# Masked attention over kept tokens: turning x into rows and outputs into columns by VectorE's 32x32 blocks instead of TensorE's transposes

## The chip, the cores and the metric

The kernel runs on one core of one Trainium2 chip. The metric is the device time of one execution in microseconds. Five engines work side by side, each through its own instructions in order: TensorE (PE; its weight loads are listed as PEld), VectorE (DVE), ScalarE (ACT), GpSimd (POOL) and SyncE (SP, which here only issues transfers). They meet through semaphores; transfers run on 16 DMA engines.

## The reference

x has 8 batches of D = 512 features by T = 1024 tokens, float32; the mask keeps about half of the tokens; Wq and Wo are 512 x 512.

```
xt = transpose(x, (0, 2, 1))
q = xt @ Wq.T                       # queries, keys and values are all q
qh = q in 8 heads of 64
scores = einsum('bhqd,bhkd->bhqk', qh, qh) / sqrt(64)
logits = (scores * cmask + (1 - cmask) * -1e30) * rmask
ctx = softmax(logits) @ qh
out = x + transpose(ctx @ Wo.T, (0, 2, 1))
```

A row whose query is masked has only zeros as logits, so its output is the mean over all tokens and the same for each such row of a batch.

## The kernel before

The path taken is `attention_of_kept_tokens` (L319). Per batch it packs the kept tokens into NK = 576 columns (five chunks of keys, c = 0..4, the last of 64; the last column stands for the mean of all tokens), computes attention on those alone, and spreads the results to all 1024 tokens at the end. A second function for masks that keep too much lies beside it and isn't run here.

Packing: `load_batch` (L387) brings x as features by tokens. `turn` (L405) makes 128 tokens into rows with four TensorE transposes into one PSUM bank, a ScalarE copy and a store to the DRAM tensor xd that GpSimd issues; `means` (L420) sums the features with ScalarE. `search` (L442, VectorE) finds for each packed column the token it comes from, `gather` (L458, GpSimd) fetches these rows from xd, `collect` (L471) turns them back to features by tokens (xc) on TensorE.

Attention: a batch has four pairs of heads, pr = 0..3, so there are 32 pairs in a row. For a pair, `project` (L492) makes q in two halves, `values` (L512) turns q into rows v and has VectorE find the largest length, which `bias_of` (L539) makes into the exponent's bias. The main loop (L1031) goes over the pairs, and in each over c: `scores` (L553) issues the score matmuls and ScalarE's exponentials, `add_up` (L583) has VectorE add up the exponentials of chunk c-1. After the last c, `attend` (L615) issues the 40 records of the product with v. In the next pair's c = 0, `invert` (L671) makes 1/sum, writes it to DRAM (row) and reads it back spread over the partitions (rb); `contexts` (L700) multiplies the result cT by rb, at c = 2 if the current pair is pr = 0, later else.

Output: in the next batch, `output` (L710) multiplies by Wo, 128 packed tokens at a time, the four pairs' cT accumulated in one bank in the order of the pairs (L718), so its fourth step needs cT of pr = 3; the rows are stored to DRAM (od). `output` 0 and 1 are tasks of pr = 0, 2 and 3 of pr = 1, 4 of pr = 2. `fetch` (L788, GpSimd) then brings a row of od for each of the 1024 tokens (g), and `finish` (L799) turns four 128 x 128 blocks on TensorE, VectorE adds x (xr, from `load_rest`, L767) and SP stores the sum. The last batch has functions of its own (`begin_output`, `end_output`, `fetch_last`, `finish_tokens`).

The order on each engine is the order in which the program issues work. `tasks_of` (L840) gives each pair a list of further work with rough costs; `mix` (L880) merges a front and a back list, and the loop (L1070) pulls tasks so that each c gets its share:

```
for c in range(NC):
    scores(pair, c)
    if c: add_up(pair, c - 1)
    ...                        # invert, contexts, bias_of, search, gather, loads, fetch
    while todo and ... done < share * (c + 1) - 0.3 ...:
        cost, task = todo.pop(0); task(); done += cost
    issue_stores()
attend(pair)
```

Before, `turn` for the next batch stands in the lists of pr = 0 (five) and pr = 1 (three, first of all), `finish` of the batch before in the list of pr = 3, and `search` in the c loop of pr = 0. PSUM banks for all this come from one ring of four (`bank`, L379); scores have two tiles of two banks.

Of the kernel before, what the change touches and what calls it, by code (L numbers as in the profile page):

```python
# [10 lines left out]
F32 = mybir.dt.float32  # L11
I32 = mybir.dt.int32
AF = mybir.ActivationFunctionType
ALU = mybir.AluOpType
AX = mybir.AxisListType
# [6 lines left out]
Q = 32  # L22
NK = 576
# [295 lines left out]
def attention_of_kept_tokens(ctx, tc, x, mask, wq, wo, out, ident, wqT, woT, verdict, flag):  # L319
# [24 lines left out]
    nc = tc.nc  # L344
    B, D, T = x.shape
    P = 128
    DK = D // NH
    SCALE = 1.0 / math.sqrt(DK)
    ND = D // P
# [2 lines left out]
    NN = T // NB  # L352
    G = NB // P
    A = P // Q
    KH = NK // 2
    sizes = [min(P, NK - c * P) for c in range(-(-NK // P))]
    NC = len(sizes)
# [10 lines left out]
    key = keep.tile([P, NC], F32, name="key")  # L368
    kept = keep.tile([P, B], F32, name="kept")
    origin = keep.tile([P, B, NT], I32, name="origin")  # L370
    pads = keep.tile([P, B, NC], F32, name="pads")
    pens = keep.tile([P, B, NC], F32, name="pens")
    low = keep.tile([P, 2, LAST], F32, name="low")
# [5 lines left out]
    def bank(name):  # L379
        return ps.tile([P, NB], F32, tag="t", name=name, bufs=4)  # L380


    weights = {}
    xs, xbars, xds, xins, xcs, valids, searches = {}, {}, {}, {}, {}, {}, {}
    stores = [[], []]

    def load_batch(b, queue=None):  # L387
        xs[b] = {}
        for r in range(NN):
            for d in range(ND):  # L390
                t = sb.tile([P, NB], F32, tag="x", name=f"x_{b}_{d}_{r}", bufs=NN * ND)
                (queue or nc.sync).dma_start(t, x[b, d * P : (d + 1) * P, r * NB : (r + 1) * NB])
                xs[b][d, r] = t

    def queries_of(b):

# [5 lines left out]
            nc.gpsimd.tensor_copy(part[rows, :], valid[rows, r * KH : (r + 1) * KH])  # L402
        valids[b] = valid, part

    def turn(b, i):  # L405

        r, at = divmod(i * P, NB)
        pt = bank(f"xt_{b}_{i}")
        for d in range(ND):
            nc.tensor.transpose(pt[:, d * P : (d + 1) * P], xs[b][d, r][:, at : at + P], ident)  # L410
        if i == 0:
            xds[b] = dr.tile([T, D], F32, tag="xd", name=f"xd_{b}")
            xbars[b] = sb.tile([P, ND, NN], F32, tag="xbar", name=f"xbar_{b}")
        xt = sb.tile([P, D], F32, tag="xt", name=f"xt_{b}_{i}", bufs=5)
        nc.scalar.copy(xt, pt)  # L415
        nc.gpsimd.dma_start(xds[b][i * P : (i + 1) * P, :], xt)  # L416
        if i % G == G - 1 and b:
            means(b, r)

    def means(b, r):  # L420
        for d in range(ND):
            to = xbars[b][:, d, r : r + 1]
            if b:
                junk = sb.tile([P, NB], F32, tag="junka", name=f"junka_{b}_{r}_{d}", bufs=1)
                nc.scalar.activation(junk, xs[b][d, r], AF.Copy, accum_out=to)  # L425
            else:
                nc.vector.tensor_reduce(to, xs[b][d, r], axis=AX.X, op=ALU.add)

    def place_ranks(b):
        rank = sb.tile([P, T], F32, tag="rank", name=f"rank_{b}", bufs=1)  # L430
# [40 lines left out]
    def collect(b, i):  # L471
        n = sizes[i]
        if i == 0:
            xcs[b] = sb.tile([P, ND, NK], F32, tag="xc", name=f"xc_{b}", bufs=1)
        xin = xins[b][i]
        pt = bank(f"xc_{b}_{i}")
        for d in range(ND):
            nc.tensor.transpose(  # L478
                pt[:, d * n : (d + 1) * n], xin[:n, d * P : (d + 1) * P], ident[:n, :n]
            )  # L480
        nc.scalar.copy(
            xcs[b][:, :, i * P : i * P + n], pt[:, : ND * n].rearrange("p (d n) -> p d n", d=ND)
        )
        if i == LAST:
            mean = sb.tile([P, ND], F32, tag="mean", name=f"mean_{b}")
            nc.vector.tensor_tensor(mean, xbars[b][:, :, 0], xbars[b][:, :, 1], ALU.add)
            nc.vector.tensor_scalar(xcs[b][:, :, NK - 1], mean, 1.0 / T, None, ALU.mult)


    qTs, vs, tops, biases = {}, {}, {}, {}  # L490
# [244 lines left out]
    def begin_output(b, i):  # L735

        n = sizes[i]
        po = bank(f"pa_{b}_{i}")
        for pr in range(ND - 1):
            nc.tensor.matmul(  # L740
                po[:n, :],
                cTs[b, pr][:, i * P : i * P + n],
                woT[:, pr, :],
                start=(pr == 0),
                stop=(pr == ND - 2),
            )
        pa = sb.tile([P, D], F32, tag="xt", name=f"pa_{b}_{i}", bufs=5)
        nc.scalar.copy(pa[:n, :], po[:n, :])
        partials[i] = pa

    def end_output(b, i):
# [12 lines left out]
        nc.vector.tensor_tensor(oc[:n, :], po[:n, :], partials[i][:n, :], ALU.add)  # L764
        nc.sync.dma_start(ods[b][places[i], :], oc[:n, :])

    def load_rest(b):  # L767
        for r in range(NN):
            for d in range(ND):
                xr = sb.tile([P, NB], F32, tag="xr", name=f"xr_{b}_{r}_{d}", bufs=NN * ND)  # L770
                nc.sync.dma_start(xr, x[b, d * P : (d + 1) * P, r * NB : (r + 1) * NB])
                xrs[b, r, d] = xr

    def fetch_last(b):

# [12 lines left out]
    def fetch(b):  # L788
        for i in range(NT):
            g = sb.tile([P, D], F32, tag="g", name=f"g_{b}_{i}", bufs=NT)  # L790
            nc.gpsimd.indirect_dma_start(  # L791
                out=g,
                out_offset=None,
                in_=ods[b],
                in_offset=bass.IndirectOffsetOnAxis(ap=origin[:, b, i : i + 1], axis=0),
            )
            gs[b, i] = g

# [11 lines left out]

    def load_rest_of_tokens(b):

        for i in range(NT):
            xr = sb.tile([P, ND, P], F32, tag="x", name=f"xr_{b}_{i}", bufs=NN * ND)
            nc.sync.dma_start(
                xr, x[b, :, i * P : (i + 1) * P].rearrange("(d p) t -> p d t", p=P)
            )
            xrs[b, i] = xr

    def finish_tokens(b, i):  # L820
        xr = xrs.pop((b, i))
# [18 lines left out]
    def tasks_of(p):  # L840

        b, pr = pairs[p]
        first, front, back, end = [], [], [], []
        if p + 2 < len(pairs):
            ahead = pairs[p + 2]
            front = [(2.0, lambda hf=hf: project(ahead, hf)) for hf in range(2)]
            front.append((0.6, lambda: values(ahead)))
            if p == 0:
                behind = pairs[1]
                front = [  # L850
                    (2.0, lambda: project(behind, 1)),
                    (0.6, lambda: values(behind)),
                    front[0],
                    (0.3, lambda: bias_of(behind)),
                    *front[1:],
                ]
        if p == ND - 1:
            back = [(0.5, lambda d=d: turn_weights(woT, "wo", d)) for d in range(ND)]
        if b + 1 < B:
            if pr < 2:  # L860
                mine = range(0, 5) if pr == 0 else range(5, NT)
                turns = [(0.5, lambda i=i: turn(b + 1, i)) for i in mine]
                if pr == 0:
                    back += turns
                else:
                    first = turns
            if pr == 2:
                front = [(0.5, lambda i=i: collect(b + 1, i)) for i in range(NC)] + front
        if b > 0:
            if pr < 3:  # L870
                mine = {0: (0, 1), 1: (2, 3), 2: (4,)}[pr]
                (back if pr else end).extend((3.6, lambda i=i: output(b - 1, i)) for i in mine)
            elif b + 1 < B:
                t = 0.5
                back += [(t, lambda r=r, d=d: finish(b - 1, r, d)) for r in range(NN) for d in range(ND)]
        if p + 1 == len(pairs):
            end = [(2.7, lambda i=i: begin_output(b, i)) for i in range(NC)]
        return first + mix(front, back) + end

    def mix(front, back):  # L880

# [26 lines left out]
    def early():  # L908
# [94 lines left out]
        for i in range(NC):  # L1003
            search(0, i)
        for i in range(NT):
            turn(0, i)
        for r in range(NN):
            means(0, r)
        pt = bank("home_t")
        nc.tensor.transpose(pt[:, :BC], home, ident[:BC, :BC])  # L1010
        nc.vector.tensor_copy(origin, pt[:, :BC].rearrange("p (b c) -> p b c", c=NT))

    def late():
        weights["wq"] = load_weights(wq, "wq")
# [13 lines left out]
        project(pairs[1], 0)  # L1028
        bias_of(pairs[0])

        for p, pair in enumerate(pairs):  # L1031
            b, pr = pair
            before = pairs[p - 1] if p else None
# [3 lines left out]
            for c in range(NC):  # L1037
# [15 lines left out]
                if 0 < p < len(pairs) - 1 and c == 1:  # L1053
                    bias_of(pairs[p + 1])
                if b + 1 < B:
                    if pr == 0:
                        search(b + 1, c)
                        if c == 1:
                            queries_of(b + 1)
                    if pr == 1 and c == LAST:  # L1060
                        for i in range(NC):
                            gather(b + 1, i)
# [4 lines left out]
                    load_rest(b - 1)  # L1067
                if pr == 3 and c == 0 and b > 0:
                    fetch(b - 1)
                while todo and (c or p + 1 < len(pairs)) and (done < share * (c + 1) - 0.3 or c == LAST):  # L1070
                    cost, task = todo.pop(0)
                    task()
                    done += cost
# [126 lines left out]
```

## Time and profile before

| what | value |
|---|---|
| three runs, median (range) | 771.29 us (770.23 to 773.01) |
| profiled execution: its own time / its span | 769.13 us / 767.4 us |
| granted TensorE clock, mean over the span | 0.985 |
| chain that ended last, on PE / ACT / DVE | 79% / 5% / 5% |
| its shares on PE lines: scores, av, pq, po | 19%, 17%, 15%, 13% |
| its shares on PE lines: xt (turn), o (finish) | 3%, 3% |
| turn's transposes (L410) / finish's (L803) | 256 / 224 of 128x128 |
| batch 3, pair 3 / batch 4, pair 0, from the end of av to the next | 19.0 us / 24.5 us |

The busy time says how much an engine did; the chain says what set the end. PE's share of the chain is spread over all its matmuls in proportion, which is how a span bound by one in-order engine looks. Where the words "pair 3" and "pair 0" stand below, the pairs pr = 3 and the following pr = 0 of the next batch are meant.

### The profile page before, as it was taken

The numbers are of one execution on the slowest core, as the hardware profiler recorded it, in microseconds if no ns is written. First come the engines' busy times: TensorE is split into PE (matmuls) and PEld (weight loads), VectorE is DVE, ScalarE is ACT, GpSimd is POOL, SyncE is SP. The second block draws the span as 40 slices with busy tenths as digits, with TensorE's granted clock in tenths as the row PEclk, the third lists the DMA queues.
The fourth block names the chain that finished last, engine by engine and source line by source line (L and its number), as shares of the span: only waits on it lengthen the run. The fifth ranks groups of instructions, "written<-read, shape, count | busy, mean of one in ns | idle before, by whom it ended". The sixth has DMA issues, their size and how long they took to land.

```text
span 767.4 us, 12722 instructions
## 1 busy us (share of the span) xinstructions
PE 721.3 (94%) x4411; PEld 425.1 (55%) x4411; DVE 496.1 (65%) x1495; ACT 386.8 (50%) x783; POOL 200.7 (26%) x264
## 2 busy tenths in 40 slices
PE   6699999999999999999999999999999999899883
PEld 5565565555655556556655556555655566354342
DVE  6287767556975668556984569656785567547453
ACT  3376566644465546545466545645476544245400
POOL 4723003134112413134031432134031340003221
PEclk9899999999999999999999999999999999999996
DMA  7543402556226843447235653357335342146238
GB/s 266 169 166 117 159 18 101 196 165 228 93 108 205 254 166 108 158 144 262 101 141 182 224 195 115 88 207 251 139 128 172 124 135 88 61 155 170 74 128 268
DMA packets 59098, 119.52 MB, mean 156 GB/s; under 512 B 10144, under 2 KB 18400, under 8 KB 59024
## 3 DMA queue, kind: packets, MB, share of 16 engines
q1 hardware_dynamic: 37792, 61.55, 24.2%
q0 software_dynamic: 17008, 54.97, 21.1%
q10 hardware_dynamic: 4224, 2.10, 0.9%
q8 instruction: 37, 0.61, 0.3%
q14 instruction: 37, 0.30, 0.1%
HBM read 75.40 MB, written 43.18 MB: 155 GB/s over the span
## 4 chain that ended last, share of the span: by engine, by line
PE 79%; ACT 5%; DVE 5%; another core or an unknown queue 3%; DMA 3%; issue 2%; POOL 1%; ACTq 0%; POOLq 0%; DVEq 0%
PE s L570 19%; PE av L607 17%; PE pq L501 15%; PE po L720 13%; PE xc L478 4%; PE xt L410 3%; PE o L803 3%; ACT e L574 3%; PE v L520 2%; PE pa L740 2%; DVE junk L591 1%; DMA rank<-ranks 1%; DMA g<-od,origin 1%; ACT v L523 1%
## 5 line engine op out<-in xcount | busy, mean ns | idle before, releaser
L591 DVE CUSTOM_DVE_ANT_0 junk<-e,valid 128x576 f32<-128x576 f32 x256 | 194.9, 761 | 122.4 <-ACT e L574 117.7
L570 PE MATMUL s<-qT 64*128 64x288 f32 (+1 forms) x1280 | 186.3, 434 | 10.6 <-ACT e L574 9.7
L574 ACT ACTIVATE e<-s,bias 128x576 f32<-128x576 f32 x256 | 176.1, 740 | 34.2 <-PE s L570 23.3
L570 PEld LDWEIGHTS s<-qT 64*128 64x128 f32 (+1 forms) x1280 | 93.7, 175 | 97.1 <-issue 58.5
L501 PE MATMUL pq<-xc,wqT 128*128 128x288 f32 x512 | 138.9, 414 | 0.5 <-issue 0.5
L607 PE MATMUL av<-e,v 128*64 128x288 f32 x1024 | 132.6, 409 | 0.8
L720 PE MATMUL po<-woT,cT 128*128 128x512 f32 (+1 forms) x336 | 117.3, 532 | 2.3 <-DVE cT L703 2.3
L501 PEld LDWEIGHTS pq<-xc,wqT 128*128 128x128 f32 x512 | 92.2, 190 | 34.6 <-issue 8.1
L416 POOL DMA_DIRECT2D xd<-xt x64 | 35.5, 558 | 251.3 <-ACT xt L415 250.9
L607 PEld LDWEIGHTS av<-e,v 128*64 128x64 f32 x1024 | 71.0, 137 | 53.5 <-issue 7.2
L623 ACT COPY cT<-av 128x288 f32<-128x288 f32 x62 | 22.3, 401 | 144.5 <-PE av L607 95.3
L720 PEld LDWEIGHTS po<-woT,cT 128*128 128x128 f32 (+1 forms) x336 | 48.2, 173 | 54.7 <-issue 44.1
L729 POOL DMA_DIRECT2D od<-oc x42 | 23.1, 550 | 199.7 <-ACT oc L727 199.7
L791 POOL DMA_INDIRECT g<-od,origin x56 | 59.6, 1065 | 46.0 <-issue 15.7
L508 ACT COPY qT<-pq 128x288 f32<-128x288 f32 x64 | 25.4, 397 | 67.0 <-PE pq L501 64.6
L528 DVE TENSOR_TENSOR sq<-v 128x640 f32<-128x640 f32 x32 | 26.3, 823 | 43.0 <-ACT v L523 36.7
L727 ACT COPY oc<-po 128x512 f32<-128x512 f32 (+1 forms) x35 | 19.2, 550 | 57.0 <-PE po L720 57.0
L463 POOL DMA_INDIRECT xin<-xd,source x40 | 41.6, 1039 | 18.5 <-issue 9.4
L451 DVE TENSOR_SCALAR_CACHE_REDUCE junk<-rank,key 128x1024 f32<-128x1024 f32 (+4 forms) x40 | 40.1, 1002 | 4.1 <-DMA rank<-ranks 2.7
L806 DVE TENSOR_TENSOR xr<-o,xr 128x512 f32<-128x512 f32 x56 | 36.4, 684 | 5.1 <-PE o L803 2.6
L415 ACT COPY xt<-xt 128x512 f32<-128x512 f32 x64 | 35.4, 591 | 2.4 <-PE xt L410 2.1
L425 ACT ACTIVATE junka<-x 128x512 f32<-128x512 f32 x56 | 35.7, 637 | 1.3
(131 smaller groups left out, 698.6 us busy)
## 6 DMA issues: line engine op xcount, KB each, us to landing
xd<-xt POOLq DMA_DIRECT2D x64, 256.0 KB
xr<-in_x_dram SPq DMA_DIRECT2D x64, 256.0 KB
x<-in_x_dram SPq DMA_DIRECT2D x56, 256.0 KB
out_dram<-xr SPq DMA_DIRECT2D x56, 256.0 KB
rb<-row SPq DMA_DIRECT2D x60, 160.0 KB
od<-oc POOLq DMA_DIRECT2D x28, 256.0 KB
rank<-ranks SPq DMA_DIRECT2D x6, 512.0 KB
x<-in_x_dram POOLq DMA_DIRECT2D x8, 256.0 KB
```

What stands on the lines that cost most here:

```text
L416: nc.gpsimd.dma_start(xds[b][i * P : (i + 1) * P, :], xt)
L425: nc.scalar.activation(junk, xs[b][d, r], AF.Copy, accum_out=to)
L451: nc.vector.tensor_scalar(junk[:, :n], rank[:, i * P :], key[:, col], 0.0, ALU.is_le, ALU.add, accum_out=found[:, col])
L463: nc.gpsimd.indirect_dma_start(out=xin[:n, :], out_offset=None, in_=xds[b], in_offset=bass.IndirectOffsetOnAxis(ap=searches[b][2][:n, i : ...
L501: nc.tensor.matmul(pq[:, :KH], wqT[:, d, pr * P : (pr + 1) * P], xcs[b][:, d, cols], start=(d == 0), stop=(d == ND - 1),)
L570: nc.tensor.matmul(s[to, h, :KH], qT[heads[h], keys], qT[heads[h], queries], start=True, stop=True)
L574: nc.scalar.activation(e[:, hf if c < LAST else 0, :, :], s[:, :, :KH], AF.Exp, bias=biases[pair][:, c : c + 1], scale=SCALE,)
L591: nc.vector.tensor_tensor_reduce(junk[:, :n].rearrange("p (f k) -> p f k", k=KH), e[:, :, h, :], (valid if c < LAST else part).rearrange(" ...
L607: nc.tensor.matmul(av[head, :KH], v[keys, c, head], e[keys, hf if c < LAST else 0, h, :], start=(c == 0), stop=(c == LAST),)
L720: nc.tensor.matmul(po[k * n : (k + 1) * n, :w], cTs[b, pr][:, i * P : i * P + n], woT[:, pr, k * w : (k + 1) * w], start=(pr == 0), stop=( ...
L791: nc.gpsimd.indirect_dma_start(out=g, out_offset=None, in_=ods[b], in_offset=bass.IndirectOffsetOnAxis(ap=origin[:, b, i : i + 1], axis=0),)
L806: nc.vector.tensor_tensor(xr, pt, xr, ALU.add)
```

## The change

For batches 1 to 7 `turn` no longer uses TensorE, ScalarE and GpSimd. x is loaded with partition p holding features 4p to 4p+3, in two tiles of 128 x 4 x 512. One VectorE instruction turns 256 tokens as 32x32 blocks (128 x 1024 elements); SP stores them to xd in four transfers, one for each quadrant of 32 partitions, with the 32 tokens outermost and pieces of 128 floats. There are four such turns for a batch, at (pr, c) = (0,0), (0,2), (0,4), (1,1). Sums of features are one ScalarE instruction at each of the first eight c; `mean_of` sends them through DRAM to bring them into the order of the features. Batch 0 keeps TensorE (`turn_first`). `search` moves from pr = 0 to pr = 1.

For batches 0 to 5 `finish` becomes `finish_blocks`: eight times per batch VectorE turns one fetched tile g (128 x 512) by blocks and adds xr. `fetch` takes other tokens for this (block_origin, from `place_blocks`), xr is one tile of 32 features per quadrant, loaded and stored in four transfers each. The eight stand at (3,2), (3,3), (3,4), two each, and (0,0), (0,1) of the next batch, one each; the stores follow at pr = 0. Batch 6 keeps TensorE's finish, at the end, and batch 7 its own.

The diff at its core:

```
+    def turn(b, i):
+        n = T // NQ
+        r, at = divmod(i * n, NB)
...
+        xt = sb.tile([P, n // Q, P], F32, tag="xt", name=f"xt_{b}_{i}", bufs=2)
+        nc.vector.transpose(
+            xt.rearrange("p k (f d) -> p k d f", d=ND),
+            xs[b][r][:, :, at : at + n].rearrange("p d (k t) -> p k d t", t=Q),
+        )
+        def store():
+            for a in range(A):
+                to = xds[b][i * n : (i + 1) * n, a * P : (a + 1) * P]
+                nc.sync.dma_start(
+                    to.rearrange("(k t) c -> t k c", t=Q), xt[a * Q : (a + 1) * Q, :, :]
+                )
+        stores[1].append(store)
...
+    def mean_of(b):
+        total = sb.tile([P, ND], F32, tag="total", name=f"total_{b}")
+        nc.vector.tensor_tensor(total, xbars[b][:, :, 0], xbars[b][:, :, 1], ALU.add)
+        xmeans[b] = sb.tile([P, ND], F32, tag="mean", name=f"mean_{b}")
+        row = dr.tile([P, ND], F32, tag="mean", name=f"mean_row_{b}")
+        nc.sync.dma_start(row, total)
+            nc.sync.dma_start(xmeans[b], row.rearrange("(a f) d -> (f d) a", a=A))
...
+    def finish_blocks(b, i):
+        o = sb.tile([P, D // Q, Q], F32, tag="o", name=f"o_{b}_{i}", bufs=2)
+        nc.vector.transpose(o.rearrange("p k t -> p (k t)"), gs[b, i])
+        xr = xrs[b]
+        to = xr[:, :, i * Q : (i + 1) * Q]
+        nc.vector.tensor_tensor(to, o, to, ALU.add)
+        if i == NT - 1:
+            def store():
+                for a in range(A):
+                    nc.sync.dma_start(in_blocks(out[b])[a], xr[a * Q : (a + 1) * Q, :, :])
+            stores[0].append(store)
...
-            if pr < 2:
-                mine = range(0, 5) if pr == 0 else range(5, NT)
-                turns = [(0.5, lambda i=i: turn(b + 1, i)) for i in mine]
...
-            elif b + 1 < B:
-                t = 0.5
-                back += [(t, lambda r=r, d=d: finish(b - 1, r, d)) for r in range(NN) for d in range(ND)]
...
+        TURN = [(0, 0), (0, 2), (0, 4), (1, 1)]
+        FINISH = {
+            (ND - 1, 2): (0, 1),
+            (ND - 1, 3): (2, 3),
+            (ND - 1, 4): (4, 5),
+            (0, 0): (6,),
+            (0, 1): (7,),
+        }
...
                 if b + 1 < B:
-                    if pr == 0:
+                    if (pr, c) in TURN:
+                        turn(b + 1, TURN.index((pr, c)))
+                    if pr < 2 and pr * NC + c < NN * ND:
+                        add_features(b + 1, pr * NC + c)
+                    if pr == 1 and c == LAST:
+                        mean_of(b + 1)
+                    if pr == 1:
                         search(b + 1, c)
...
+                for i in FINISH.get((pr, c), ()):
+                    of = b - 1 if pr == ND - 1 else b - 2
+                    if of in BLOCKS and of >= 0:
+                        finish_blocks(of, i)
```

Also: `load_rest_of_tokens` for the last batch loads rows of 512 tokens where it loaded pieces of 128, and the last batch's partial outputs use another tile tag.

## The prediction

> **What bounds the kernel now.** I read the page's first part, then the chain, then the busy times by stretch, then the order of time on DVE and PE around one place. First the shares, and two stretches of the span: pair 3 of batch 3 and pair 0 of batch 4 (columns: stretch, length, busy us of PE, PEld, DVE, ACT, POOL, granted clock, DMA share, GB/s).
>
> ```profile
> PE 721.3 (94%) x4411; PEld 425.1 (55%) x4411; DVE 496.1 (65%) x1495; ACT 386.8 (50%) x783; POOL 200.7 (26%) x264
> 360.00:379.00 19.00, 18.87 (x138) 12.29 (x134) 14.56 (x37) 8.38 (x16) 0.49 (x1) 1.00 0.36 129
> 379.00:403.50 24.50, 24.50 (x142) 13.97 (x138) 20.79 (x66) 14.84 (x31) 6.88 (x10) 1.00 0.30 112
> ```
>
> PE has no gap, so each TensorE instruction taken out shortens the span. But DVE is full here too: 35.4 us of work in 43.5 us, against 65% in the mean. What the removed transposes take is read from the chain (start, us, what), here o in pair 3 and xt in pair 0, and the output matmul that comes later:
>
> ```profile
> 364.79 1.31 PE o L803 x12
> 382.39 0.87 PE xt L410 x8
> 389.81 3.65 PE po L720 x8
> ```
>
> Now DVE in order of time (start, us, line, operation, what it waited for): the first add_up of pair 3, three of finish's adds, contexts from its first to its last instruction in pair 0, and the small transpose that ends invert.
>
> ```profile
> 363.61 0.76 DVE L591 CUSTOM_DVE_ANT_0 junk<-e,valid 128x576 f32<-128x576 f32 x1 [3.57 <-ACT e L574]
> 365.74 1.88 DVE L806 TENSOR_TENSOR xr<-o,xr 128x512 f32<-128x512 f32 x3
> 381.35 0.21 DVE L677 STREAM_TRANSPOSE rt<-ris 128x32 f32<-128x32 f32 x1
> 389.32 0.23 DVE L695 TENSOR_TENSOR rb<-rb 128x64 f32<-128x64 f32 x1 [0.59 <-DMA rb<-row]
> 391.45 0.15 DVE L704 COPY cT<-qT 128x1 f32<-128x1 f32 x1
> ```
>
> The reader is to see a tight meeting: contexts of pair 3 ends at 391.6, and output 0 on PE (389.81 to 393.46) needs it for its last quarter, at 392.5. One microsecond is spare. DVE's sequence to it is fixed by the program.
>
> **The change part by part.** Out of PE: per batch four pieces of xt in the chain (0.87 + 0.44 + 1.03 in pair 0, 1.46 in pair 1 = 3.8 us) for seven batches, 26.5 us; five pieces of o in pair 3 (1.31 + 0.59 + 1.02 + 0.59) for six batches, 21.1 us. Together 47.6 us. Out of ACT and POOL: 56 copies of 591 ns and 56 issues of 558 ns, worth nothing by themselves, since ACT is 50% and POOL 26% busy.
>
> Into DVE: 28 turns and 48 pairs of transpose and add. The only transpose in the trace is the 128x32 one, 212 ns. Other DVE rows grow by one element per 1.0 to 1.1 ns (TENSOR_TENSOR 128x512 684 ns, 128x640 823 ns). With 480 elements more, 128x512 takes 0.71 us and 128x1024 1.25 us (estimates). From below, no DVE row of 512 elements advances its engine by less than 0.61 us; from above I let each further element cost twice, 1.21 and 2.3 us. I take the low slope, as 212 ns for 32 elements leaves little room for the other. The add advances by 0.63 us (three in 1.88). So one finish is 0.71 + 0.03 + 0.63 = 1.37 us (1.2 to 1.9), where the old one was 0.63.
>
> [...]
>
> Now the walk, from 360.06, the start of pair 3. PE without o: 19.0 - 3.5 = 15.5 us to the end of the pair. Then pair 0, whose tasks are now both project halves, values and the outputs: s 1.17, pq 2.14 and 1.94, s 1.17, top 0.25, v 0.55, s 1.17, three quarters of po 2.74: 11.1. So PE wants the last cT at 26.6.
>
> DVE: first e at 3.55 (363.61). Pair 3: four add_ups of 1.48, bias 0.65, contexts 2.20, sq to top 1.78, last add_up with inverses 2.00, six finishes of 1.37: 12.5 + 8.2. That ends at 24.3; before it ended at 21.3, though PE was 3.5 us later then. Pair 0, in its new order: turn 1.25, finish 6, add_up 1.48, bias 0.65, finish 7, sq to top 1.78, add_up 1.48, contexts 2.20: 8.85 + 2.75. cT of pair 3 is ready at 35.9. The searches, which stood here, are gone to pair 1 and that is counted.
>
> PE stands at output 0 for 35.9 - 26.6 = 9.3 us. Behind the waiting matmul stand all scores of c = 3 and 4 and av, hence ACT's exponentials. rb isn't late: before, it came 7.8 us after invert, now 7.8 us after 24.3 is 32.1, ahead of contexts at 33.7. What follows (48 us after 360.06 pair 0 ends) leaves DVE time to catch up: two turns, two add_ups and inverses, 7.5 us, in some 11. Six batches meet this (2 to 7): 56 us. In batch 1 no finish is ahead of it, but DVE must take sq after ACT's copy of v: about 3 us late.
>
> The idle PE then loses clock. After the stretch 16.0 to 24.5, in which PE did nothing, it shows this (same columns as above):
>
> ```profile
> 16.00:24.50 8.50, 0.00 (x0) 0.00 (x0) 5.03 (x11) 1.16 (x2) 4.40 (x6) 0.78 0.54 181
> 24.50:26.00 1.50, 1.24 (x6) 1.27 (x7) 0.00 (x0) 0.12 (x1) 1.11 (x2) 0.50 0.71 188
> 26.00:27.50 1.50, 1.50 (x9) 1.50 (x8) 0.00 (x0) 1.05 (x2) 1.24 (x2) 0.50 0.74 216
> ```
>
> Three microseconds at half clock cost 1.5 us, six times: 9 us (bounds 0 and 9).
>
> The rest: search in pair 1 (6 us with its small operations) with the last turn (1.25) makes DVE there some 20.4 of PE's 22.1; it ends about 4 us behind av, but the next thing PE takes from it, top, comes 5 us into pair 2 and is earlier in DVE's order. If that cover fails, it costs up to 2 us a batch. mean_of adds two transfers in a row on SP, issued at the end of pair 1; the mean is used 9.9 us into pair 2 (now 171.16 against 161.2), two landings like row to rb take 7.8. place_blocks is 16 copies of some 0.16 us once, in pair 2, where DVE is 12.4 of 20 us busy.
>
> Transfers: SP gains 16 issues for xd per batch and loses none of its row and rb; each issue takes 0.4 to 0.6 us (128 and 512 pieces: medians 507 and 636 ns), and the stores stand behind rb in the queue, so rb isn't held up. xd moves in 512-byte pieces. Two queues' rows (packets, MB, share of 16 engines):
>
> ```profile
> q0 software_dynamic: 17008, 54.97, 21.1%
> q10 hardware_dynamic: 4224, 2.10, 0.9%
> ```
>
> q10 is the last batch's 512-byte stores: 0.9% of 767.4 us is 6.9 us for 2.1 MB, 3.3 us per MB; q0 takes 161.9 us for 55 MB, 2.9 per MB. So small pieces cost a tenth more, hidden: a batch's xd is needed some 20 us after its last turn's issue, xr and out a batch later. Bounds 0 and 2 us a batch.
>
> [...]
>
> Sum: 769.1 - 47.6 + 56 + 3 + 9 = 789.5; the profiled run is 2.2 below the median of the three, so up to 791 in their terms. I name 789.
>
> **The rivals.** A, the transposes are hidden: DVE's work lies beside PE's everywhere and PE stays the only bound: 769.1 - 47.6 + 2.2 = 724. For it: DVE has 35% free in the mean. Against it: the free time lies in pairs 1 and 2, and the one-microsecond meeting. It decides where the wait at output 0, per batch, is below about 6 us with the clock loss, 7.4 without: a finish of 0.95 or 1.13 us, below every DVE row. B, half of it: DVE's operations overlap more than I add up, the wait is 4.5 us and too short to slow the clock: 769.1 - 47.6 + 27 + 3 = 751. For it: adds already overlap by 0.06 us. C, gain and wait cancel: 769 to 773. D, the blocks cost double: finish 1.9 us adds 0.5 x 8 x 6 = 24, turn 6: 819; the same if the quadrant transfers hold up pair 2 by a few us a batch.
>
> **How the numbers follow.** My forecast 0.60, A 0.12, B 0.13, C 0.07, D 0.08. The forecast's own range is 770 to 815: 9 less without clock loss, 7 less at the low bound of finish, 24 more at the high one. The range for eight in ten leaves out A and D: 750 to 815. Within 0.3% (2.3 us; what this measurement can tell from no change) is C's 0.07; faster is A and B, 0.25; slower 0.68.
>
> **What would show it.** After: a group "PE po" with a wait on DVE's cT of about 9 us in six batches; STREAM_TRANSPOSE rows of about 0.71 and 1.25 us; pair 3 about 15.5 us long, pair 0 about 32; granted clock 0.5 after the wait. I am wrong if PE shows no wait at output 0 (A), if the transposes are far off 0.71 us, or if PE waits at xc for xin, or at top.

## The result and the profile after

| | us |
|---|---|
| before, median of 4 runs (range) | 770.76 (766.55 to 773.01) |
| after, median of 4 runs (range) | 826.44 (823.84 to 828.80) |
| ratio after / before (95% interval) | 1.0728 (1.0668 to 1.0789) |
| profiled execution after: time / span | 828.80 / 827.0 |
| granted TensorE clock, mean: before / after | 0.985 / 0.925 |

The change makes the kernel 7.3% slower. The direction was forecast, the size was not: 826 lies above the range that ended at 815.

First the page's busy times of the changed kernel, then pair 3 of batch 3 and the pair 0 behind it, cut at the ends of av (columns as in the prediction: stretch, length, busy us of PE, PEld, DVE, ACT, POOL, granted clock, DMA share, GB/s).

```profile
PE 706.8 (85%) x3995; PEld 393.5 (48%) x3995; DVE 583.5 (71%) x1582; ACT 358.6 (43%) x727; POOL 169.3 (20%) x208
```

```profile
288.93:305.02 16.09, 15.51 (x104) 8.82 (x106) 12.55 (x30) 8.47 (x17) 0.63 (x1) 1.00 0.28 103
305.02:339.37 34.35, 24.93 (x120) 12.66 (x122) 29.85 (x71) 12.71 (x29) 3.25 (x5) 0.85 0.51 133
```

PE was busy 94% of its span and is now busy 85%: 416 matmuls are gone, and yet the span is 59.6 us longer, so PE waits. Pair 3 got shorter (19.0 to 16.1 us), pair 0 longer (24.5 to 34.4 us), with 9.4 us in it in which PE does nothing. What it waits for stands in the view of waits (what waited, for what; total us, times, longest):

```profile
PE po L764 <- DVE cT L747: 57.3, 7, 9.8
...
PE xc L524 <- DMA xin<-xd,source: 30.7, 9, 9.2
...
PE xc L524 <- ACT e L618: 3.3, 1, 3.3
```

These are two waits, not one. The first is the forecast one at output 0. The second, at the first transposes of collect in pair 2, waits for gathered rows; 9.2 us of it is the kernel's start and stood in the trace of before as well, so 24.8 us are new (30.7 + 3.3 - 9.2; the line that names ACT is the same place in one more batch). In the order of time on PE, one of each kind:

```profile
325.59 2.08 PE L764 MATMUL po<-woT,cT 128*128 128x512 f32 x2 [9.42 <-DVE cT L747]
...
367.22 1.09 PE L524 MATMUL xc<-ident,xin 128*128 128x128 f32 x4 [4.14 <-DMA xin<-xd,source]
```

The price of the new VectorE instructions, from the groups by shape (count, then busy us and mean ns of one):

```profile
L446 DVE STREAM_TRANSPOSE xt<-x 128x1024 f32<-128x1024 f32 x28 | 57.5, 2054 | 0.3 <-issue 0.3
L841 DVE STREAM_TRANSPOSE o<-g 128x512 f32<-128x512 f32 x48 | 33.7, 702 | 0.0
L844 DVE TENSOR_TENSOR xr<-o,xr 128x512 f32<-128x512 f32 x48 | 33.2, 692 | 1.7
```

A finish costs what was estimated (0.70 + 0.69 us). A turn costs 2.05 us, near the upper of its two bounds.

Why xin is late in pair 2 is read from the queue of SP and then from POOL, in the order of time:

```profile
350.35 1.85 SPq L454 DMA_DIRECT2D xd<-xt  x4
352.25 2.13 SPq L829 DMA_DIRECT2D xr<-in_x_dram  x4
360.39 0.34 SPq L471 DMA_DIRECT2D mean_row<-total  x1
368.81 0.39 SPq L473 DMA_DIRECT2D mean<-mean_row  x1
```

```profile
357.90 1.03 POOL L509 DMA_INDIRECT xin<-xd,source  x1 [0.55 <-DVE cT L748]
```

Right behind the last store of xd (0.5 MB in 512-byte pieces) SP issues the load of xr (2 MB in 1-KB pieces). The first gather is issued at 357.90 and its rows are used from 367.2 on, 9.3 us later; before, a gather issued at 246.38 was used at 251.67, 5.3 us later, without a wait. The small mean_row, issued at 360.39, is held up in the same way: the read that waits for it leaves at 368.81.

### The profile page after: what moved, and what is told of

Same layout as the page of the kernel before. It is cut to its first block, busy times and chain, and to the rows that moved or that the text cites. A ratio compares the mean times of both kernels' runs of the same rounds, so it can differ in the third digit from the quotient of the medians.

```text
span 827.0 us, 11782 instructions
## 1 busy us (share of the span) xinstructions
PE 706.8 (85%) x3995; PEld 393.5 (48%) x3995; DVE 583.5 (71%) x1582; ACT 358.6 (43%) x727; POOL 169.3 (20%) x208
## 4 chain that ended last, share of the span: by engine, by line
PE 49%; DVE 32%; DMA 9%; issue 5%; ACT 2%; SPq 1%; POOL 1%; DVEq 0%; POOLq 0%; another core or an unknown queue 0%; ACTq 0%
PE s L614 12%; PE po L764 11%; PE av L651 10%; PE pq L545 8%; DVE junk L635 7%; DMA xin<-xd,source 7%; DVE o L841 4%; DVE xr L844 4%; DVE xt L446 3%; PE xc L524 3%; DVE junk L497 2%; PE pa L784 2%; DVE len L574 2%; ACT e L618 2%; DVE sq L572 2%
## 5 line engine op out<-in xcount | busy, mean ns | idle before, releaser
L614 PE MATMUL s<-qT 64*128 64x288 f32 (+1 forms) x1280 | 194.0, 448 | 7.4 <-ACT e L618 6.0
L618 ACT ACTIVATE e<-s,bias 128x576 f32<-128x576 f32 x256 | 176.6, 739 | 34.6 <-PE s L614 24.5
L764 PE MATMUL po<-woT,cT 128*128 128x512 f32 (+1 forms) x336 | 135.3, 615 | 57.3 <-DVE cT L747 57.3
L614 PEld LDWEIGHTS s<-qT 64*128 64x128 f32 (+1 forms) x1280 | 96.8, 182 | 104.6 <-issue 62.3
L764 PEld LDWEIGHTS po<-woT,cT 128*128 128x128 f32 (+1 forms) x336 | 53.3, 199 | 120.4 <-DVE cT L747 63.1
L870 POOL DMA_INDIRECT g<-od,block_origin x48 | 53.1, 1105 | 31.2 <-issue 28.2
L446 DVE STREAM_TRANSPOSE xt<-x 128x1024 f32<-128x1024 f32 x28 | 57.5, 2054 | 0.3 <-issue 0.3
L589 DVE TENSOR_REDUCE m<-top 128x1 f32<-128x128 f32 x32 | 9.3, 290 | 66.4 <-PE top L587 66.4
L524 PE MATMUL xc<-ident,xin 128*128 128x128 f32 (+1 forms) x160 | 24.2, 294 | 34.0 <-DMA xin<-xd,source 30.7
L635 DVE CUSTOM_DVE_ANT_0 junk<-el,part 128x288 f32<-128x288 f32 x64 | 29.1, 454 | 13.2 <-ACT el L618 12.0
```

The source lines that it names most:

```text
L446: nc.vector.transpose(xt.rearrange("p k (f d) -> p k d f", d=ND), xs[b][r][:, :, at : at + n].rearrange("p d (k t) -> p k d t", t=Q),)
L524: nc.tensor.transpose(pt[:, d * n : (d + 1) * n], xin[:n, d * P : (d + 1) * P], ident[:n, :n])
L614: nc.tensor.matmul(s[to, h, :KH], qT[heads[h], keys], qT[heads[h], queries], start=True, stop=True)
L618: nc.scalar.activation(e[:, hf if c < LAST else 0, :, :], s[:, :, :KH], AF.Exp, bias=biases[pair][:, c : c + 1], scale=SCALE,)
L635: nc.vector.tensor_tensor_reduce(junk[:, :n].rearrange("p (f k) -> p f k", k=KH), e[:, :, h, :], (valid if c < LAST else part).rearrange(" ...
L764: nc.tensor.matmul(po[k * n : (k + 1) * n, :w], cTs[b, pr][:, i * P : i * P + n], woT[:, pr, k * w : (k + 1) * w], start=(pr == 0), stop=( ...
```

## The experiments

Runs of one group ran on one chip and share its runs of the kernel before. These took 758.5, 769.8, 758.9 and 768.8 us in the four groups, so kernels of different groups are compared by their ratio to before. The expectations are in microseconds of the chip above, on which before takes 771.

| run | group | ratio to before (95%) | PE waits for cT at output 0 | PE waits for xin, without the 9.0 to 10.5 us at the start |
|---|---|---|---|---|
| changed kernel again | 2 | 1.0783 (1.072 to 1.0845) | 57.6 | 24.9 |
| xr loaded later | 1 | 1.1116 (1.1093 to 1.114) | 43.7 | 1.6 |
| outputs later | 1 | 1.0274 (1.0254 to 1.0295) | 0 | 25.2 |
| finish on TensorE | 1 | 1.0183 (1.0161 to 1.0204) | 20.2 | 3.5 |
| turn on TensorE | 1 | 1.0242 (1.0214 to 1.027) | 20.4 | 0 |
| turn writes side by side | 2 | 1.0712 (1.0653 to 1.0772) | 53.5 | 22.0 |
| xr in whole rows | 2 | 1.0415 (1.0351 to 1.048) | 57.4 | 2.6 |
| rebalanced | 2 | 1.0389 (1.0325 to 1.0453) | 0.6 | 3.0 |
| outputs later and xr in whole rows | 3 | 0.9832 (0.9814 to 0.9851) | 0 | 3.7 |
| rebalanced, transfers spread | 3 | 1.006 (1.0021 to 1.01) | 37.7 | 2.7 |
| the same, rb ahead | 4 | 0.9841 (0.9803 to 0.9879) | 16.9 | 2.3 |

Three of these kernels time a part and leave out the right result: in "turn writes side by side" the features of a token lie in another order, and in the two with xr in whole rows x is added in other places than it belongs.

### The two halves of the change

Finish back on TensorE (the tasks of before in pair 3, xr and out by rows), turn as changed:

```
-    BLOCKS = range(B - 2)
+    BLOCKS = range(0)
...
+        if b > 0 and pr == 3 and b + 1 < B:
+            back += [(0.5, lambda r=r, d=d: finish(b - 1, r, d)) for r in range(NN) for d in range(ND)]
```

> Half of the change: turn by VectorE's blocks with the quadrant stores of xd stays; finish goes back to TensorE in pair 3, and xr and out are loaded and stored by rows of 512 tokens as before the change. Theory 1 (the wait at output 0 is made by the finishes, the wait at xc by the quadrant load of xr): both waits are below 1.5 us, 26 us of xt are saved, and the time is 745 to 765, faster than before. Theory 2 (the wait at xc is made by the quadrant stores of xd): it stays at 3 to 4 us and costs 5 us a batch: 775 to 790. In both the turn stays at 2.05 us.

Turn back on TensorE, ScalarE and GpSimd, as `turn_first`, with x loaded by rows of features for all batches; finish as changed:

```
-        nc.vector.transpose(
-            xt.rearrange("p k (f d) -> p k d f", d=ND),
-            xs[b][r][:, :, at : at + n].rearrange("p d (k t) -> p k d t", t=Q),
-        )
...
+        for d in range(ND):
+            nc.tensor.transpose(pt[:, d * P : (d + 1) * P], xs[b][r][:, d, at : at + P], ident)
+        nc.scalar.copy(xt, pt)
+        nc.gpsimd.dma_start(xds[b][i * P : (i + 1) * P, :], xt)
```

> The other half: finish by VectorE's blocks with quadrant loads of xr and stores of out stays; turn goes back to TensorE, ScalarE and GpSimd (rows of 2 KB stored to xd), the sums need no detour through DRAM, and search stays in pair 1. Theory 1: the wait at output 0 shrinks by the one turn on VectorE (2.05 us) and by some 2.3 us of xt that TensorE has again in pair 0, to about 5 us; the wait at xc stays at 3 us or more because the quadrant load of xr is still ahead of the gathers; time 800 to 825. Theory 2 (the wait at xc is made by the stores of xd): it is gone here and the time is 775 to 795.

The waits of PE, first with finish on TensorE, then with turn on TensorE:

```profile
PE po L764 <- DVE cT L747: 20.2, 7, 2.9
PE xc L524 <- DMA xin<-xd,source: 13.5, 6, 10.0
```

```profile
PE po L746 <- DVE cT L729: 20.4, 6, 7.0
PE xc L506 <- DMA xin<-xd,source: 9.5, 1, 9.5
```

Each half alone is slower than before, by 1.8% and 2.4%; together they cost 7%. The wait at output 0 falls from 57 to 20 us in both. The wait at xc is gone in both, apart from the start: with xr by rows, though xd is stored by quadrants, and with xd by rows, though xr is loaded by quadrants. So neither theory had it right. But the second half takes away more than the small stores of xd. The load of xr and the first gather behind it, with turn on TensorE, and then in the kernel before:

```profile
318.49 2.13 SPq L811 DMA_DIRECT2D xr<-in_x_dram  x4
335.88 1.03 POOL L491 DMA_INDIRECT xin<-xd,source  x1 [0.38 <-issue]
```

```profile
229.72 5.09 SPq L771 DMA_DIRECT2D xr<-in_x_dram  x8
246.38 1.03 POOL L463 DMA_INDIRECT xin<-xd,source  x1 [0.38 <-issue]
```

There the load leaves 17 us ahead of the gather. In the changed kernel it leaves 5.6 us ahead (352.25 and 357.90), because it stands on SP's queue behind the last store of xd, which waits for the last turn on VectorE (348.19 to 350.3). So the halves point to a load of xr in quadrants that is in flight together with the gathers, which the next section tests; whether the small pieces of xd add to the wait is not shown.

The first half saves 26 us of xt and is still 13 us slower than before on its chip. Against the trace of the kernel before with a span of 756.3 us it waits 18 us more at output 0 and 5 us more at xc, and po and s take 12 us longer, at a clock of 0.966 in the mean.

### Where xr is loaded

```
-                if pr == 1 and c == 2 and b > 0:
+                if pr == 2 and c == 3 and b > 0:
                     load_rest(b - 1)
```

> The changed kernel with only one thing moved: xr of the batch before is loaded at (pr 2, c 3) instead of (pr 1, c 2), so it no longer stands between the last store of xd and the gathers of xin. Theory 1 (the xr load, 2 MB in 1-KB pieces by quadrants, fills the DMA engines while the gathers are in flight, so their landing takes 9.2 us and the first transpose of collect on PE waits 3.7 us and loses clock after it): the landing falls to about 5 us, the wait at xc to below 1 us, and six batches save 3.7 to 6 us each: 826.4 becomes 790 to 805; the wait at output 0 stays 9 to 10 us. Theory 2 (xd itself is late, because its last turn stands behind the bias on VectorE and goes out in 512-byte pieces): the wait at xc stays above 3 us and the time 822 to 830.

The wait at xc went as theory 1 said, and the kernel became slower than the changed one. Waits of this kernel:

```profile
PE top L587 <- DVE top L581: 57.6, 7, 12.2
...
DVE xr L844 <- DMA xr<-in_x_dram: 47.2, 5, 12.3
```

At its new place the load stands behind 2.5 MB of x and ranks and ahead of row and rb. One such load took SP 11.1 us to issue (379.65 to 390.72), row could be issued only behind it, and the first finish in pair 3 stood up to 12 us on VectorE for xr. Here the moved transfer took its wait along.

The same load at its old place, in another shape:

```
-            for a in range(A):
-                nc.sync.dma_start(xr[a * Q : (a + 1) * Q, :, :], in_blocks(x[b])[a])
+            for r in range(4):
+                nc.sync.dma_start(
+                    xr.rearrange("p k n -> p (k n)")[:, r * T : (r + 1) * T], x[b, r * P : (r + 1) * P, :]
+                )
```

> The changed kernel with the load of xr (2 MB at the same place, pr 1, c 2) as four loads of 128 partitions by 4 KB instead of four quadrants of 32 partitions in pieces of 1 KB; xd and out are stored by quadrants as in the changed kernel. x is then added in other places than it belongs. Theory 1 (it is the small pieces: 2 MB of them take 10 us or more where whole rows take 6, and the gathers behind them land late): the wait at xc falls from 3.7 us to below 1 us, the time by 15 to 30 us against the changed kernel, and the wait at output 0 stays at 9 to 10 us. Theory 2 (any 2 MB ahead of the gathers do this, or it is the stores): the wait at xc stays above 3 us and the time within 5 us of the changed kernel.

The ten microseconds behind the issue of xr, in the changed kernel of the same group and then in this one (columns as above):

```profile
350.00:355.00 5.00, 5.00 (x31) 2.38 (x31) 4.72 (x16) 1.97 (x4) 1.25 (x2) 1.00 1.03 203
355.00:360.00 5.00, 4.46 (x38) 2.19 (x34) 4.83 (x15) 0.40 (x1) 3.78 (x5) 1.00 1.14 201
```

```profile
340.00:345.00 5.00, 5.00 (x25) 2.13 (x25) 4.76 (x14) 2.17 (x5) 0.54 (x1) 1.00 0.99 315
345.00:350.00 5.00, 5.00 (x46) 2.74 (x44) 4.83 (x15) 0.47 (x2) 3.71 (x4) 1.00 0.89 313
```

The DMA engines are full in both (share 0.9 to 1.1), but move 202 GB/s in quadrants with 1-KB pieces and 314 GB/s in 128 partitions with 4 KB. That is enough: the wait at xc falls from 24.9 to 2.6 us and the ratio from 1.078 to 1.042, with the wait at output 0 unchanged. Theory 1 holds. This run changes the length of the pieces and the number of partitions together; which of them sets the rate was not tried.

### The meeting at output 0

VectorE's order is left alone; TensorE asks later:

```
-            mine = {0: (0, 1), 1: (2, 3), 2: (4,)}[pr]
+            mine = {0: (), 1: (0, 1, 2), 2: (3, 4)}[pr]
```

> The changed kernel with outputs 0 to 2 as tasks of pair 1 and outputs 3 and 4 of pair 2, so that TensorE doesn't need cT of pair 3 before pair 1. VectorE's work and its order are not touched. Theory 1 (TensorE stands at output 0 for 9.4 us in six batches because six finishes, a turn, finish 6 and 7 lie ahead of contexts on VectorE, and then runs some 5 us at half clock): that wait goes, 57 us and 6 to 15 us of clock, 826.4 becomes 752 to 770. Theory 2 (VectorE is full from pair 3 on, so TensorE only waits at the next place that needs VectorE, the bias of a later pair or output 0 in pair 1): most of the wait comes back under another name and the time stays above 795.

```profile
PE xc L524 <- DMA xin<-xd,source: 34.6, 9, 9.4
PE top L587 <- DVE top L581: 18.7, 12, 1.9
PE s L614 <- ACT e L618: 13.3, 40, 0.4
```

The wait at output 0 is gone altogether, and with it 4.5 to 5.1% of the time of the kernel before (1.0274 against 1.0728 and 1.0783). What is left is the untouched wait at xc, and small waits at top and at the exponentials, 32 us in all, because VectorE is without a gap from pair 3 to the end of pair 1 (4.7 to 4.9 us of each 5) and then half idle in pair 2 (17.3 us busy in the 35 from 340 to 375). So theory 1 names the place, and theory 2 why the gain stays below 57 us. One of the four timed runs took 1669 us; it isn't in the ratio and wasn't explained.

Both moves in one kernel, outputs later and xr in whole rows:

> Two of the moves at once in the changed kernel: outputs 0 to 2 in pair 1 and 3 and 4 in pair 2, and the load of xr in whole rows (x is then added in other places than it belongs). Theory 1 (the wait at output 0 and the wait at xc are two separate losses): both are gone and their gains add up, 5 per cent from the one and 3.7 from the other: ratio 0.985 to 1.0. Theory 2 (VectorE is full from pair 3 to pair 1 anyway, and the wait at xc only let it catch up): without it the waits at top and at the exponentials grow, and the ratio is 1.01 to 1.03.

```profile
PE top L587 <- DVE top L581: 17.9, 12, 1.9
PE xc L524 <- DMA xin<-xd,source: 14.2, 5, 10.5
PE s L614 <- ACT e L618: 13.3, 40, 0.4
```

The two gains add up and a little more (0.983, where the two alone make 0.991), and the waits at top and at the exponentials are what they were with one move. They were two separate losses. The trace of the kernel before from this group (its single time was 758.13 us, span 756.3) also shows what the waits did to the clock (in the mean 0.975 here, 0.983 there and 0.925 in the changed kernel): without them po takes 114.5 us here against 117.7 there and s 185.8 against 184.3, where the changed kernel shows 135.3 and 194.0. pq is longer here, 144.2 us against 138.5.

### The price of a turn

```
-            xt.rearrange("p k (f d) -> p k d f", d=ND),
+            xt.rearrange("p k (d f) -> p k d f", d=ND),
```

> Only the order in which a turn writes its 1024 floats is changed: each 32x32 block to 32 floats next to each other, where the changed kernel writes single floats 16 bytes apart. The features of a token then lie in another order in xd, so this kernel computes the attention of reordered features; every other instruction is as in the changed kernel. Theory 1 (the price of 2.05 us comes from the spacing of the written floats): the turn's row falls to 1.25 to 1.45 us, one turn is on the path to output 0, whose wait falls from 9.5 to 8.7 us, and the time falls by 4 to 8 us against the changed kernel. Theory 2 (a transpose of 1024 elements costs 2 us in any order): the row stays at 2.0 us and the time is within 2 us of the changed kernel.

```profile
L446 DVE STREAM_TRANSPOSE xt<-x 128x1024 f32<-128x1024 f32 x28 | 34.8, 1242 | 0.3 <-issue 0.3
```

1.24 us against 2.07: 0.8 us of a turn is the spacing of its writes, and the estimate of 1.25 us was right for writes side by side. The median fell by 6.6 us, from 828.05 to 821.44.

### Rearranging without undoing

The rebalanced kernel keeps all blocks on VectorE and moves only places:

```
-            mine = {0: (0, 1), 1: (2, 3), 2: (4,)}[pr]
+            mine = {0: (0,), 1: (1, 2), 2: (3, 4)}[pr]
...
+        TURN = {(0, 0): 2, (0, 3): 3}
+        TURN_AHEAD = {(ND - 1, 1): 0, (ND - 1, 3): 1}
...
+            (0, 3): (0,), (0, 4): (1,), (1, 1): (2,), (1, 3): (3,), (2, 0): (4,), (2, 1): (5,), (2, 2): (6, 7),
...
+                if pr == 3 and c == 2 and b > 0:
                     load_rest(b - 1)
...
+                nc.scalar.dma_start(xr[a * Q : (a + 1) * Q, :, :], in_blocks(x[b])[a])
```

> Both kinds of transposes stay on VectorE; only places are changed, after what the first four runs showed. VectorE was full in pairs 3, 0 and 1 and half idle in pair 2, and the transfers in small pieces filled the DMA engines in pairs 0 and 1. So: two turns of the batch after next in pair 3, two in pair 0, all ahead of pair 1; finishes behind contexts in pair 0 (two), in pair 1 (two) and pair 2 (four); out stored in pair 2 and xr loaded in pair 3, both from ScalarE's queue so that row and rb don't stand behind them; output 0 at the end of pair 0, 1 and 2 in pair 1, 3 and 4 in pair 2. Theory 1 (what was lost were two meetings, not the work itself): VectorE has some 17, 20, 22 and 18 us in pairs 3, 0, 1 and 2 where TensorE has 15.5, 20, 23 and 24, the waits at output 0 and at xc vanish, and the time is 0.95 to 0.975 of the kernel before. Theory 2 (VectorE at nine tenths of TensorE's time, or the small transfers, can't be hidden wherever they stand): waits of 3 us or more in each batch remain at another place, and the ratio is 0.99 to 1.03.

Both old waits are gone, and in the batch looked at PE has no gap above 0.4 us in pairs 0 and 1. But the ratio is only 1.039, as ScalarE's own row shows (its DMA issues, then its next copy):

```profile
382.63 8.84 ACTq L829 DMA_DIRECT2D xr<-in_x_dram  x4
391.52 0.40 ACT L552 COPY qT<-pq 128x288 f32<-128x288 f32 x1 [8.28 <-DMA xd<-xt]
```

Issuing four quadrants in a row took 8.8 us, while SP issued eight stores of xd beside it and the DMA engines went to a share of 1.1, and ScalarE's exponentials stood behind it (PE waits for e: 52 us). The next kernel issues them on SP, one quadrant at a chunk, and loads x at pr 1:

```
+        LOAD = {(3, 2): 0, (3, 3): 1, (3, 4): 2, (0, 0): 3}
+        STORE = {(2, 3): 0, (2, 4): 1, (3, 0): 2, (3, 1): 3}
```

> The rebalanced kernel with its transfers spread: in it pairs 0 and 1 ran without a wait of TensorE, but ScalarE stood 4 us and 9 us in issuing the four transfers of out and of xr in a row, and its exponentials with it. Here these are issued by SyncE, one quadrant at a chunk (out at pr 2, c 3 and 4, and pr 3, c 0 and 1; xr at pr 3, c 2 to 4, and pr 0, c 0), x of the batch after next is loaded at pr 1 instead of pr 2, where the transfers are few, and the sums of features are all made in pair 0 for that. Theory 1 (what remained was the issue on ScalarE's queue): TensorE is the only bound, the 47 us of transposes are saved, 5 to 15 us of small waits remain: ratio 0.945 to 0.97. Theory 2 (2 MB out and 2 MB xr in small pieces fill the engines in pairs 2 and 3 and hold up row, rb or g wherever they are issued): waits of 3 us and more remain in each batch, ratio above 0.985.

It came to 1.006, above 0.985 as theory 2 said, with one large wait left, at output 0: 6.2 to 8.4 us in four batches, 2.1 and 3.9 us in two. SP's queue ahead of one of them:

```profile
369.58 2.57 SPq L454 DMA_DIRECT2D xd<-xt  x4
372.20 0.55 SPq L830 DMA_DIRECT2D xr<-in_x_dram  x1
374.17 3.28 SPq L724 DMA_DIRECT2D row<-rt  x4
381.22 1.09 SPq L729 DMA_DIRECT2D rb<-row  x2
```

row takes 3.28 us to issue where it takes 1.4 in a quiet stretch, and rb follows 7 us later instead of 2.4, so contexts, and output 0 behind it, are late. The last kernel puts two of the quadrants behind row and rb, takes the other transfers out of that place, and moves a turn and the finishes a little:

```
+        LOAD = {(3, 2): 0, (3, 3): 1, (0, 1): 2, (0, 2): 3}
+        STORE = {(2, 3): (0,), (2, 4): (1, 2), (3, 0): (3,)}
+        TURN_AHEAD = {(2, 3): 0, (ND - 1, 1): 1}
```

> The spread kernel with one queue conflict taken out: in it the only wait left was at output 0, 8 us in five batches, because row and rb of pair 3 stood on SyncE and on the DMA engines behind three quadrants of xr and two stores of xd (row issued 3.3 us long, rb 7 us later than else). Now two quadrants of xr go at pr 3, c 2 and 3, and two at pr 0, c 1 and 2, behind row and rb; out goes at pr 2, c 3 and 4, and pr 3, c 0; the first turn of a batch stands at pr 2, c 3, the second at pr 3, c 1; the finishes one place later. Theory 1 (the order of the transfers was what remained): the wait at output 0 falls below 2 us a batch, and the ratio is 0.94 to 0.965, below both kernels. Theory 2 (the transfers of a batch can't be placed without meeting row and rb somewhere): a wait of 4 us or more appears again in each batch, at output 0, top or xc, ratio 0.98 to 1.01.

```profile
PE po L764 <- DVE cT L747: 16.9, 5, 6.4
PE s L614 <- ACT e L618: 14.0, 28, 4.2
PE xc L524 <- DMA xin<-xd,source: 11.4, 4, 9.1
```

It takes 756.63 us (753.62 to 760.3) where before takes 768.84: 0.9841 (0.9803 to 0.9879). It beats both kernels, by less than theory 1 said; the ratio is one that theory 2 named. Waits at output 0 are still 16.9 us, two of them above 4 us, and of the 47 us of removed transposes 12 arrive.

The changed kernel as it is, for the groups' comparison, came out nearly as expected: five waits at output 0 of 9.5 to 9.8 us and the last of 6.9, and waits at xc of 3.6 to 4.5 us:

> The changed kernel as it is, for a reference on the same chip as the next ones: ratio to the kernel before 1.06 to 1.08, turn 2.05 us, six waits at output 0 of 9 to 10 us, waits at xc of 3.3 to 4.2 us in batches 2 to 7.

And the kernel before, for its trace:

> The kernel before, for its trace on the same chip as the next two: ratio 1.00, no wait of TensorE between 60 and 700 us above 2 us.

Its single time is 758.13 us beside a median of 758.94. Between 60 and 700 us it has one wait above 2 us, 2.3 us at output 0 of the last batch but one.

## Why the prediction was right in kind and wrong in size

The profiled executions differ by 59.7 us, the spans by 59.6. The new trace splits them so:

| term | predicted | shown | from |
|---|---|---|---|
| transposes taken from PE | -47.6 | -47.0 | PE busy -14.5, less the growth below |
| wait for cT at output 0 | +59 | +55.0 | 57.3 - 2.3 |
| wait for xin at xc | 0 (bound: 2 a batch) | +24.8 | 30.7 + 3.3 - 9.2 |
| PE lines that stayed, longer | +9 (as clock) | +32.5 | po +18.0, s +7.7, xc +2.4, others +4.4 |
| other waits | 0 | -5.7 | rest of PE's idle time (+74.1) |
| sum | +20.4 | +59.6 | |

Removed work: right as far as can be told. The -47.0 is a remainder and not a measurement of its own; but in pair 3 PE's busy time fell from 18.87 to 15.51 us, by 3.4 where 3.5 were forecast.

The walk to output 0: right nearly to the instruction. In the stretch that begins at 288.93, PE wants the last cT at 27.2 us (predicted 26.6), invert ends at 24.6 (24.3), and contexts ends at 36.8 (35.9); the wait is 9.4 (9.3). The wait is this near by some luck, as both its ends came late, PE's by 0.6 us and the release by 0.8. Of the 0.9 us in contexts 0.3 was there at invert, and the turn, which kept VectorE 1.9 us (313.48 to 315.40), makes the rest. Batch 1 waits 2.94 us (predicted 3). The mechanism is confirmed: moving the outputs alone removes the whole wait.

Price of a finish: right (0.70 and 0.69 us). Price of a turn: 2.05 us where 1.25 was taken; the argument "the low slope" was right for a transpose that writes side by side (1.24 us) and left out that each turn writes its floats 16 bytes apart. That cost 6.6 us, the difference between the medians of the kernels with the two kinds of turn.

The step that failed is the one on transfers: "small pieces cost a tenth more, hidden". It priced each transfer by its bytes, from one queue's row (3.3 against 2.9 us per MB), and asked how long after its issue it was needed. It didn't ask what else is in flight then, nor what the stores of xd, which now wait for VectorE, hold up behind them on SP's queue: it looked at rb alone, and the load of xr left 5.6 us ahead of the first gather where before it left 16.7. For the "some 20 us" from the last turn's issue to the need of xd, the trace shows 7.5 us to the first gather (350.35 to 357.90). In them 2.6 MB in quadrants are issued (4 x 128 KB and 4 x 512 KB), and at 202 GB/s, the rate of this stretch in a second run of the kernel, these take 13 us. Four quadrants in flight moved at that rate, where whole rows moved at 314 GB/s. The bound of 2 us a batch was passed: 3.4 to 4.1 us in six batches, 24.8 us in all, and the clock behind it. The prediction named this very wait as what would prove it wrong, and rival D named quadrant transfers that hold up pair 2, at 0.08. That xr in flight beside the gathers is the cause is shown by two runs: without it there (loaded later), or with it in whole rows, the wait is gone.

The clock term was mis-sized. "Three microseconds at half clock" was read from a stretch that began when PE started again. Read microsecond by microsecond, the half clock begins inside a long wait and goes on after it. The same place of before, then the wait of the changed kernel that ends at 226.3, then one of the waits of 2.9 us with finish on TensorE, which ends at 392.6 (columns as above; the last but two is the clock):

```profile
20.00:21.00 1.00, 0.00 (x0) 0.00 (x0) 1.00 (x4) 0.00 (x0) 0.00 (x0) 0.84 0.00 0
21.00:22.00 1.00, 0.00 (x0) 0.00 (x0) 0.03 (x1) 0.00 (x0) 0.89 (x1) 0.50 0.00 0
...
26.00:27.00 1.00, 1.00 (x7) 1.00 (x6) 0.00 (x0) 0.73 (x2) 0.78 (x1) 0.50 0.66 205
27.00:28.00 1.00, 1.00 (x9) 1.00 (x8) 0.00 (x0) 0.73 (x2) 0.96 (x2) 0.75 0.73 229
```

```profile
221.00:222.00 1.00, 0.00 (x0) 0.00 (x0) 0.96 (x2) 0.00 (x0) 0.00 (x0) 0.77 0.38 105
222.00:223.00 1.00, 0.00 (x0) 0.00 (x0) 0.97 (x3) 0.00 (x0) 0.00 (x0) 0.50 0.85 189
...
231.00:232.00 1.00, 1.00 (x2) 0.35 (x2) 0.56 (x1) 1.00 (x3) 0.00 (x0) 0.61 0.90 186
232.00:233.00 1.00, 1.00 (x4) 0.41 (x3) 0.97 (x5) 0.01 (x1) 0.00 (x0) 1.00 0.97 207
```

```profile
394.00:395.00 1.00, 1.00 (x8) 0.52 (x4) 1.00 (x2) 0.84 (x2) 0.37 (x1) 0.61 0.00 0
...
397.00:398.00 1.00, 1.00 (x3) 0.49 (x2) 0.98 (x3) 0.00 (x0) 0.00 (x0) 0.69 0.92 272
```

The slices inside a stretch show 0.50 and those outside it 1.00, so a mean of 0.84 over a microsecond means that the clock fell 0.68 us into it. So the first stretch runs from 20.68 to 27.5, 6.8 us, of which 3 came after the wait; the second from 221.54 to 231.78, 10.2 us, of which 5.5 came after it. The third is 3.4 us long and lies wholly behind its wait (394.22 to 397.62). All stretches at the waits at output 0 and at xc of these two kernels are 3.4, 6.8 or 10.2 us long, and between 60 and 740 us the clock falls nowhere else in them. The length of the wait alone doesn't decide which comes: a wait of 3.35 us at xc lost no clock, and six of the seven waits of 2.5 to 3.0 us with finish on TensorE did, though rival B called 4.5 us too short for it.

Read so for every wait of the changed kernel, PE runs at half clock for 27.9 us behind the six waits at output 0, 6.3 us behind the one of batch 1, and 21.9 us behind five of the six at xc (one of them from 367.2 to 371.7). Half of these 56 us is 28 us, an estimate that takes PE as busy throughout; the lines that stayed grew by 32.5. The prediction counted six waits and 3 us behind each. With both waits absent (outputs later and xr in whole rows) most of the growth is absent too.

Hidden work that was indeed hidden: search in pair 1 (PE waits for top 1.5 us in the whole run), place_blocks, and the stores of out. mean_of was called free and is, for PE, though SP stood up to 10 us with it.

## What to carry to other kernels

Work that moves from a full engine to a half idle one should be placed by stretches: the order of the receiving engine up to the next meeting decides, and here moving the meeting alone gave back some 5%. Transfers that are split into pieces need a count of all bytes in flight in the stretch before their first use, at the rate that such pieces were measured to have (here 202 GB/s, against 314 for whole rows). A wait of a few microseconds on TensorE can cost more than itself: in the changed kernel 12 of 13 waits of 2.9 us or more at output 0 and xc were followed by 3.4 to 6.3 us at half clock.

## What the runs showed of the hardware

- A VectorE 32x32 transpose of 1024 floats a partition takes 1.24 us with writes side by side and 2.07 us with single floats 16 bytes apart; 512 floats take 0.70 us.
- DMA engines with a share of about 1 moved 202 GB/s while xr came in quadrants with 1-KB pieces, and 314 GB/s while it came in 128 partitions with 4-KB pieces.
- An engine that issues transfers can stand in it: four quadrants of xr took SP 11.1 us behind 2.5 MB of other loads, and ScalarE 8.8 us beside eight stores of xd, against 2.1 us in the changed kernel.
- The half clock came in stretches of 3.4, 6.8 and 10.2 us, and 6.8 us even where PE had waited only 2.95 us (302.1 to 308.9 with finish on TensorE).
